# Keys and values of the context made beside the first scans instead of in the tail of a Mamba, MLP, attention and LoRA kernel

## The chip, the cores and the metric

The kernel runs on one core of a Trainium2 chip. The core has five engines with queues of their own: TensorE (PE, with weight loads shown as PEld), VectorE (DVE), ScalarE (ACT), GpSimd (POOL) and SyncE (SP), which here only issues transfers. The metric is the device time of one execution in microseconds (us). The profile is of one execution; L311 in it is the line of a helper through which most instructions go, so that groups are told apart by the names of their tiles.

## The reference

The input is x, 4 sequences of 1024 tokens and 512 channels (4096 tokens in all), and a context of 64 tokens for each sequence. One decoder layer with three parts is computed in float32, with a residual and a layer norm behind each part. Cut to what matters:

```python
h   = x + mamba(rmsnorm(x))                  # in_proj, conv, dt, B, C; the scan below; out_proj
mlp = silu(xn @ w1.T) * (xn @ w2.T) @ w3.T   # xn = rmsnorm(h)
x   = layernorm(x + h + mlp)
# scan of mamba, for 1024 inner channels d and 16 states n:
#   h[t] = exp(dt[t,d] * A[d,n]) * h[t-1] + dt[t,d] * B[t,n] * u[t,d];   y[t,d] = sum_n h[t] * C[t,n]
K = ctx @ Wk.T + bk;  V = ctx @ Wv.T + bv    # 16 heads of 32
Q = x @ Wq.T + bq;    qk = Q K^T
t = exp(clip(mlp3(mean qk, max qk, variance of softmax qk)))    # a temperature for each head
x = layernorm(x + (softmax(qk / (2 t)) V) @ Wo.T + bo)
x = layernorm(x + x @ W.T + b + top-2 mixture of 8 LoRA experts)
```

K and V hang on the context and on weights alone; nothing that the kernel computes of x goes into them.

## The kernel before

The 4096 tokens are 8 chunks of 512. Work on them comes in these stages:

1. `mamba_in`: for each chunk the rms norm, the input projections, the convolution, dt, B, C and the gate. Its outputs (dt, dt times u, u, the gate, B, C) go to device memory.
2. `scan_mlp`: the scans. A *group* is half a chunk's inner channels (4 tiles of 128), and a *step* k is one of the 16 states n of a group, so that there are 256 steps: group 0 is steps 0 to 15, group 1 steps 16 to 31. A step has four *quarters* (`quarter(k, q, other)`). In quarter q DVE runs the scan of tile q of step k, ACT the exponent for the scan two quarters later (`exp`), PE transposes 128 tokens of step k - 1 into a PSUM bank (`turn`), and the bank is multiplied by C (`times_c`): for some (n, t) DVE adds it to an accumulator `acc`; for the others ACT writes it to a tile of its own (`hc`, or `hz` in the first two groups), which POOL adds later, or PE adds when it transposes back (`join`). In quarters 0 and 1 POOL makes the products with B for step k + 1 (`times_b`, tile `hs`). SP loads the row b of step k + 2 at quarter 0. `exp` has two PSUM banks, `turn` three.
3. From step 40 on, an MLP stream for chunk 0 and the later chunks runs on PE in `other`'s place, at a fixed pace. The first four steps (EARLY_STEPS) have the end of `mamba_in` there; from step 4 to step 39 that place is empty (`lambda: None`).
4. After the last step comes the MLP of the last chunk (`last()`), advanced by `alone`, and woven with it, turn by turn, the generator `Attention.start`, which makes ready for attention: constants, keys, values, the query weights, and then the scores of the first blocks.
5. `Attention.run`: the attention and the LoRA part, 256 tokens at a time, in an order written out by hand (`CP`).

The order on PE, DVE, ACT and POOL is the order of the program wherever `pin` is used as `nc` (class `InOrder`), one such order for `mamba_in` and one for `scan_mlp`. What is issued through the plain `nc` (all of SP, and in `Attention.start` everything but the matmuls) is placed by the framework's scheduler. `at(d, phase, f)` lets f run d quarters later, at phase 0 (before the turn), 1 (after it), 2 (before the scan) or 3 (at the end).

The keys and values before: `Attention.start` loads the context twice side by side (ctx2), wk, wv and bv, 3.25 MB together. For each of four blocks of key channels PE makes four matmuls over 256 columns into `ps_k`, ACT adds the bias (`kf`), ACT rounds it to the high part and DVE subtracts for the low part (`split`, tile `ks`), SP stores both parts in device memory, and DVE sums it (`ksum`). For each of the four sequences PE makes four matmuls over 512 columns into `ps_v`, DVE adds the bias (`vf`), `split` makes the two parts (`vs`), and SP stores them. A float32 matmul shows as two records in the profile. The banks are those of the MLP (`mm`, three). In front of them in PE's order stands the output projection of the last chunk (`ps_o`), behind some of them the four `turn`s of its MLP (`ps_t`), which need the rms norm of that projection: `norm_h` on DVE, `norm_sq` on ACT, the reciprocal root on POOL (`norm_r`), and `norm_x` on ACT.

The tiles `hz` of the first two groups come from a pool `b_z` of 44 buffers. Group 0 takes 36 of them and group 1 takes 38, from its first state on.

Of the kernel before, what the change touches and what calls it, by code (L numbers as in the profile page):

```python
# [19 lines left out]
P = 128  # L20
B, L, D = 4, 1024, 512
N = B * L
KD = D // P
# [261 lines left out]
def open_pool(tc, name, bufs, **kw):  # L285
    return tc.tile_pool(name=name, bufs=bufs, reuse_waits="tile", **kw)
# [40 lines left out]
class Slots:  # L327
# [5 lines left out]
    def at(self, d, phase, f, *args):  # L333
        self.due.setdefault((self.now + d, phase), []).append(lambda: f(*args))
# [357 lines left out]
    return rest()  # L692


def scan_mlp(tc, cn, a, dr, before, bx, then):

# [7 lines left out]
    with ExitStack() as ctx, ExitStack() as sx:  # L704
# [8 lines left out]

        carry = cp.tile([P, KI, NS], F32, tag="carry", name="carry")
        pks, bs, cts, accs, hcs, uzs, firsts = {}, {}, {}, {}, {}, {}, {}
        zps = []

        class Step:

# [79 lines left out]
            def times_c(self, t):  # L799

                c = cts[self.c][:, t, self.n : self.n + 1]
                ps = self.ps.rearrange("p i d -> p (i d)")
                if self.n == 0:
                    acc = accs[self.g, t] = ap.tile([P, GJ * P], F32, tag="acc", name="acc")
                    nc.scalar.activation(acc, ps, AF.Copy, scale=c)
                elif (self.n, t) in self.by_add | self.by_turn:
                    acc = accs[self.g, t]
                    if self.g < 2 and (self.n, t) in self.by_turn:
                        hc = zps[0].tile([P, GJ * P], F32, tag="hz", name="hz")
                    else:  # L810
# [351 lines left out]
        assert next(before, 0) == 0  # L1162
        bx.close()
        with ExitStack() as zx:
            zps.append(zx.enter_context(open_pool(tc, "b_z", bufs=44, side="right")))
            zps.append(
                zx.enter_context(open_pool(tc, "b_zp", bufs=2, space=PSUM, side="right"))
            )
            for k in range(EARLY_STEPS, 2 * NS + 8):
                for q in range(GJ):  # L1170
                    quarter(k, q, lambda: None)
            turned[0] = 0
# [71 lines left out]
class Attention:  # L1244
# [11 lines left out]
    def constants(self, cp):  # L1256
# [31 lines left out]
            )  # L1288
        nc.gpsimd.memset(f32(self.kbd), 0.0)

    def start(self, ctx, pin, mm):

        self.pin, self.mm = pin, mm
        nc, a, dr, pvec = self.nc, self.a, self.dr, self.cn["pvec"]
# [6 lines left out]
        self.ksum = cp.tile([P, 4, B], F32, tag="ksum", name="ksum")  # L1301
        for _ in range(7):
            yield
        with ExitStack() as kx:
            kv = self.pool(kx, "c_kv", 1)
            ctx2 = kv.tile([P, KD, B, 2, SK], F32, tag="ctx2", name="ctx2")
            wk = kv.tile([P, KD, D], F32, tag="wk", name="wk")
            wv = kv.tile([P, KD, D], F32, tag="wv", name="wv")
            bv = kv.tile([P, D], F32, tag="bv", name="bv")
            for i in range(2):  # L1310
                nc.sync.dma_start(
                    ctx2[:, :, :, i], a["ctxT"].rearrange("p k (b s) -> p k b s", b=B)
                )
            nc.sync.dma_start(wk, a["wk"])
            nc.sync.dma_start(wv, a["wv"])
            nc.sync.dma_start(bv, a["bv"].partition_broadcast(P))
            nc.sync.dma_start(self.tw1, a["tw1"])
            nc.sync.dma_start(self.tw2, a["tw2"])
            nc.sync.dma_start(self.tb3, a["tb3"].partition_broadcast(P))
            self.constants(cp)  # L1320
            nc.vector.tensor_copy(self.tw3, self.tw2[:, 66:67].to_broadcast([64, P]))
            yield
            for hb in range(4):
                ps = mm.tile([P, T], F32, tag="mm", name="ps_k")[:, 0 : B * SK]
                ps = ps.rearrange("p (b s) -> p b s", s=SK)
                for k in range(KD):
                    pin.tensor.matmul(
                        ps, wk[:, k, hb * P : (hb + 1) * P], ctx2[:, k, :, 0],
                        start=k == 0, stop=k == KD - 1,
                    )  # L1330
                kf = kv.tile([P, B, SK], F32, tag="kf", name="kf", bufs=2)
                nc.scalar.activation(kf, ps, AF.Identity, bias=pvec[:, V_BK + hb : V_BK + hb + 1])
                ks = kv.tile([P, 2, B, SK], F32R, tag="ks", name="ks", bufs=2)
                split(nc, ks[:, 0], ks[:, 1], kf)
                for i in range(2):
                    nc.sync.dma_start(dr["k"][:, :, i, hb], f32(ks[:, i]))
                nc.vector.tensor_reduce(self.ksum[:, hb], kf, AX.X, ALU.add)
                if hb % 2:
                    yield
            for b in range(B):  # L1340
                ps = mm.tile([P, T], F32, tag="mm", name="ps_v")
                for k in range(KD):
                    pin.tensor.matmul(
                        ps, ctx2[:, k, b].rearrange("p i s -> p (i s)"), wv[:, k],
                        start=k == 0, stop=k == KD - 1,
                    )
                vf = kv.tile([P, D], F32, tag="vf", name="vf", bufs=2)
                nc.vector.tensor_tensor(vf, ps, bv, ALU.add)
                vs = kv.tile([P, 2, D], F32R, tag="vs", name="vs", bufs=2)
                split(nc, vs[:, 0], vs[:, 1], vf)  # L1350
                nc.sync.dma_start(dr["v"][b], f32(vs))
# [604 lines left out]
def build(tc, a, out):  # L1956
    nc = tc.nc
    with ExitStack() as ctx:
# [41 lines left out]
        scan_mlp(tc, cn, a, dr, before, bx, lambda pin, mm: att.start(ctx, pin, mm))  # L2000
        att.rest(ctx)
        att.run()

# [70 lines left out]
```

## Time and profile before

| | us |
|---|---|
| median of three runs | 3323.96 (3316.99 to 3324.38) |
| the profiled execution | 3321.16 |
| its span, first to last instruction | 3319.4 |
| PE busy | 2993.0 (90%) |
| DVE busy | 2867.0 (86%) |
| POOL busy | 2454.5 (74%) |
| ACT busy | 2043.6 (62%) |
| mean granted TensorE clock | 0.955 |

The page cuts the span into 40 slices of 83 us each and gives each engine's busy share of a slice in tenths. `mamba_in` fills about the first six slices, group 0 and 1 of the scans lie around slices 7 to 10, the scans with MLPs go to about slice 30, and then come the last MLP and attention. PEclk is the clock that TensorE was granted, in tenths of full speed. The page's chain, followed back from the last instruction, is 38% PE, 26% DVE and 10% POOL. An instruction in an answer of the trace is given with its start, its duration, engine, line, what it writes and reads, its shape, how many were merged, and in brackets the idle time of the engine in front of it and what ended that.

### The profile page before, as it was taken

What the parts mean: (1) busy time and instruction counts of PE and PEld (TensorE: products, weight loads), DVE (VectorE), ACT (ScalarE), POOL (GpSimd) and SP (SyncE); (2) the same over time, 40 slices, a digit from 0 to 9 for tenths busy, and PEclk for the clock granted to TensorE, in tenths of its full rate; (3) what the DMA queues carried; (4) which work ended last, traced back from release to release, by engine and by line L of the source; (5) the groups of instructions that cost most, each with busy time, mean ns of one, the idle gap of its engine ahead of it and who ended that gap; (6) DMA issues with size and microseconds to landing.
All of it is one profiled execution on the core that took longest, in us unless ns stands there. A gap on an engine that the chain in (4) does not pass through costs nothing.

```text
span 3319.4 us, 47302 instructions
## 1 busy us (share of the span) xinstructions
PE 2993.0 (90%) x15768; PEld 2366.4 (71%) x15768; DVE 2867.0 (86%) x4063; ACT 2043.6 (62%) x4000; POOL 2454.5 (74%) x2153
## 2 busy tenths in 40 slices
PE   7999894677899999999999998999999998999986
PEld 5767672565686786786786786786786887998875
DVE  6888887998999999999999999999983346889887
ACT  3778788775665566665566665566652336666642
POOL 1456547898999999999999999999972215667643
PEclk9999995678999999999999999999999999999998
DMA  4677745334666666666766765765757532112010
GB/s 161 221 260 241 256 175 173 99 111 166 210 207 193 216 203 191 222 203 188 230 196 184 238 190 183 241 191 179 234 171 231 161 108 93 52 39 65 30 39 32
DMA packets 478474, 562.79 MB, mean 170 GB/s; under 512 B 46006, under 2 KB 309814, under 8 KB 477974
## 3 DMA queue, kind: packets, MB, share of 16 engines
q1 hardware_dynamic: 464406, 526.21, 49.6%
q10 hardware_dynamic: 13824, 33.56, 2.9%
q8 instruction: 125, 2.05, 0.2%
q14 instruction: 119, 0.97, 0.1%
HBM read 430.18 MB, written 129.50 MB: 169 GB/s over the span
## 4 chain that ended last, share of the span: by engine, by line
PE 38%; DVE 26%; POOL 10%; issue 6%; ACT 5%; DMA 3%; SPq 0%; ACTq 0%; POOLq 0%; DVEq 0%
DVE hs L311 11%; PE ps_ab L311 10%; PE ps_h L311 5%; PE ps_o L311 5%; POOL hs L311 5%; PE ps_m L311 5%; DVE acc L311 5%; PE ps_s L311 3%; PE ps_b L311 2%; POOL acc L311 2%; DVE g L311 1%; ACT da L311 1%; PE ps_in L311 1%; PE ps_y L311 1%; PE ps_num L311 1%
## 5 line engine op out<-in xcount | busy, mean ns | idle before, releaser
L311 DVE TENSOR_TENSOR_SCAN hs<-da,hs 128x512 f32<-128x512 f32 x1024 | 1225.3, 1217 | 19.8 <-ACT da L311 19.4
L311 POOL TENSOR_TENSOR hs<-pk,b 128x1024 f32<-128x1024 f32 x512 | 1214.1, 2387 | 23.3 <-PE ps_h L311 14.9
L311 ACT ACTIVATE da<-pk,aneg 128x512 f32<-128x512 f32 x1024 | 706.2, 690 | 632.1 <-DVE hs L311 622.0
L311 PE MATMUL ps_ab<-xn,w 128*128 128x512 f32 x3072 | 832.6, 407 | 3.4 <-DVE xs L311 3.4
L311 PE MATMUL ps_h<-ident,hs 128*128 128x128 f32 x4096 | 693.0, 291 | 129.1 <-DVE hs L311 66.1
L311 PEld LDWEIGHTS ps_h<-ident,hs 128*128 128x128 f32 x4096 | 533.4, 148 | 371.0 <-DVE hs L311 112.2
L311 PEld LDWEIGHTS ps_ab<-xn,w 128*128 128x128 f32 x3072 | 547.8, 191 | 98.9 <-DVE xs L311 4.1
L311 DVE SCALAR_TENSOR_TENSOR acc<-ps_h,c,acc 128x512 f32<-128x512 f32 x598 | 439.8, 735 | 26.1 <-PE ps_h L311 20.7
L311 PE MATMUL ps_m<-w,gs 128*128 128x512 f32 x1536 | 418.4, 409 | 6.0 <-POOL gs L311 3.5
L311 POOL TENSOR_TENSOR acc<-acc,hc 128x512 f32<-128x512 f32 x232 | 298.9, 1288 | 68.3 <-ACT hc L311 67.1
L311 PEld LDWEIGHTS ps_m<-w,gs 128*128 128x128 f32 x1536 | 275.6, 192 | 55.4 <-POOL gs L311 5.5
L311 PE MATMUL ps_o<-wo,wy 128*128 128x512 f32 x512 | 247.1, 601 | 10.0 <-DMA wy<-y 8.8
L311 POOL TENSOR_TENSOR gs<-g,gs 128x512 fp32r<-128x512 f32 x128 | 164.9, 1288 | 79.8 <-ACT gs L311 79.5
L311 PE MATMUL ps_in<-xn,wu 128*128 128x512 f32 x768 | 217.5, 433 | 0.3 <-DVE xn L475 0.2
L311 PE MATMUL ps_in<-xn,wz 128*128 128x512 f32 x768 | 193.2, 400 | 8.2 <-DVE cv L311 4.1
L311 ACT ACTIVATE hc<-ps_h,c 128x512 f32<-128x512 f32 x288 | 193.1, 671 | 3.8 <-PE ps_h L311 3.8
L311 PEld LDWEIGHTS ps_in<-xn,wu 128*128 128x128 f32 x768 | 147.4, 193 | 58.8 <-issue 23.8
L311 POOL TENSOR_TENSOR pt<-pw,pt 128x512 fp32r<-128x512 f32 x48 | 67.3, 1402 | 161.8 <-ACT pt L311 133.8
L311 PEld LDWEIGHTS ps_in<-xn,wz 128*128 128x128 f32 x768 | 143.2, 189 | 43.4 <-ACT q L311 4.6
L311 DVE SCALAR_TENSOR_TENSOR g<-g,ps_ab 128x512 f32<-128x512 f32 x128 | 87.4, 683 | 85.3 <-ACT g L311 84.7
L311 DVE SCALAR_TENSOR_TENSOR cv<-ps_in,pvec,cv 128x509 f32<-128x509 f32 (+2 forms) x192 | 143.3, 746 | 4.8
L311 POOL TENSOR_TENSOR q<-qf,q 128x256 fp32r<-128x256 f32 x64 | 47.6, 744 | 127.4 <-ACT q L311 127.3
(251 smaller groups left out, 4982.6 us busy)
## 6 DMA issues: line engine op xcount, KB each, us to landing
w<-w SPq DMA_DIRECT2D x384, 512.0 KB, 5.3
b<-b SPq DMA_DIRECT2D x256, 256.0 KB, 4.3
pk<-pk SPq DMA_DIRECT2D x64, 512.0 KB, 5.8
w<-pt SPq DMA_DIRECT2D x48, 512.0 KB, 3.1
pk<-z SPq DMA_DIRECT2D x64, 256.0 KB, 2.3
pk<-u SPq DMA_DIRECT2D x32, 512.0 KB, 3.7
pk<-r SPq DMA_DIRECT2D x32, 512.0 KB, 4.6
pk<-q SPq DMA_DIRECT2D x32, 512.0 KB, 5.3
```

Of the source, the lines that this page charges most:

```text
L311: ins = f(*args, **kw)
```

## The change

The generator `keys_values` is new. It does the work described above for keys and values, with its transfers, in `scan_mlp` in the place of `other`, one call in each quarter of steps 4 to 14. It issues through `pin`, so that its instructions stand in the scans' order. It has a PSUM bank (`b_kq`, one buffer) and a pool (`b_kv`) of its own, which are closed before step 15; `b_z` gets 36 buffers in place of 44, and a pool `b_z2` of 8, opened at step 15, serves the first 8 `hz` tiles of group 1.

The calls, counted from 0 at step 4, quarter 0: loads of the context in calls 0 and 1, of the four parts of wk in 2 to 5, bv in 6; a block of keys in calls 8, 11, 14 and 17; the four parts of wv, in the space of wk, in 20 to 23; and a sequence's values in calls 24, 28, 32 and 36, two of its four matmuls in that call and two in the next. The low parts are subtracted on POOL, where DVE did it before. Transfers: two of the context, eight of weights (two before), bv, eight stores of keys and four of values. `Attention.start` keeps as many turns as before, six of them now empty, and the rest of its work.

```diff
-        zps = []
+        zps, joined = [], [0, 0]
@@ times_c
                     if self.g < 2 and (self.n, t) in self.by_turn:
-                        hc = zps[0].tile([P, GJ * P], F32, tag="hz", name="hz")
+                        joined[self.g] += 1
+                        hz = zps[2 if self.g and joined[1] <= 8 else 0]
+                        hc = hz.tile([P, GJ * P], F32, tag="hz", name="hz")
@@ scan_mlp
-            zps.append(zx.enter_context(open_pool(tc, "b_z", bufs=44, side="right")))
+            zps.append(zx.enter_context(open_pool(tc, "b_z", bufs=36, side="right")))
...
-            for k in range(EARLY_STEPS, 2 * NS + 8):
+            with ExitStack() as kx:
+                kv = kx.enter_context(open_pool(tc, "b_kv", bufs=1, side="right"))
+                kq = kx.enter_context(open_pool(tc, "b_kq", bufs=1, space=PSUM, side="right"))
+                extra = beside(kv, kq, pin, at)
+                for k in range(EARLY_STEPS, NS - 1):
+                    for q in range(GJ):
+                        quarter(k, q, lambda: next(extra, None))
+                assert next(extra, 0) == 0
+            zps.append(zx.enter_context(open_pool(tc, "b_z2", bufs=8, side="right")))
+            for k in range(NS - 1, 2 * NS + 8):
                 for q in range(GJ):
                     quarter(k, q, lambda: None)
@@ class Attention
+    def keys_values(self, kp, kv, mm, pin, at):
+        nc, a, dr, pvec = pin, self.a, self.dr, self.cn["pvec"]
...
+        def key_bias(hb, ps, kf):
+            kf.append(kv.tile([P, B, SK], F32, tag="kf", name="kf"))
+            nc.scalar.activation(
+                kf[0], ps, AF.Identity, bias=pvec[:, V_BK + hb : V_BK + hb + 1]
+            )
+        def key_hi(kf):
+            kf.append(kv.tile([P, 2, B, SK], F32R, tag="ks", name="ks"))
+            nc.scalar.copy(kf[1][:, 0], kf[0])
+        def key_sum(hb, kf):
+            nc.vector.tensor_reduce(self.ksum[:, hb], kf[0], AX.X, ALU.add)
+        def key_lo(hb, kf):
+            f, s = kf
+            nc.gpsimd.tensor_tensor(s[:, 1], f, f32(s[:, 0]), ALU.subtract)
+            for i in range(2):
+                nc.sync.dma_start(dr["k"][:, :, i, hb], f32(s[:, i]))
+        def value_bias(ps, vf):
+            vf.append(kv.tile([P, D], F32, tag="vf", name="vf"))
+            nc.vector.tensor_tensor(vf[0], ps, bv, ALU.add)
+        def value_hi(vf):
+            vf.append(kv.tile([P, 2, D], F32R, tag="vs", name="vs"))
+            nc.scalar.copy(vf[1][:, 0], vf[0])
+        def value_lo(b, vf):
+            f, s = vf
+            nc.gpsimd.tensor_tensor(s[:, 1], f, f32(s[:, 0]), ALU.subtract)
+            nc.sync.dma_start(dr["v"][b], f32(s))
...
+        for hb in range(4):
+            ps = mm.tile([P, T], F32, tag="kv", name="ps_k")[:, 0 : B * SK]
...
+            kf = []
+            at(1, 1, key_bias, hb, ps, kf)
+            at(2, 1, key_hi, kf)
+            at(2, 2, key_sum, hb, kf)
+            at(2, 3, key_lo, hb, kf)
+            for _ in range(3):
+                yield
...
+        for b in range(B):
+            ps = mm.tile([P, T], F32, tag="kv", name="ps_v")
+            for k in range(KD):
+                nc.tensor.matmul(
+                    ps, ctx2[:, k, b].rearrange("p i s -> p (i s)"), w[k],
+                    start=k == 0, stop=k == KD - 1,
+                )
+                if k == 1:
+                    yield
+            vf = []
+            at(1, 2, value_bias, ps, vf)
+            at(2, 1, value_hi, vf)
+            at(2, 3, value_lo, b, vf)
+            for _ in range(3):
+                yield
@@ Attention.start
-            ctx2 = kv.tile([P, KD, B, 2, SK], F32, tag="ctx2", name="ctx2")
-            wk = kv.tile([P, KD, D], F32, tag="wk", name="wk")
-            wv = kv.tile([P, KD, D], F32, tag="wv", name="wv")
-            bv = kv.tile([P, D], F32, tag="bv", name="bv")
...
-            nc.sync.dma_start(wk, a["wk"])
-            nc.sync.dma_start(wv, a["wv"])
-            nc.sync.dma_start(bv, a["bv"].partition_broadcast(P))
...
             yield
-            for hb in range(4):
-                ps = mm.tile([P, T], F32, tag="mm", name="ps_k")[:, 0 : B * SK]
...
-            for b in range(B):
-                ps = mm.tile([P, T], F32, tag="mm", name="ps_v")
...
+            for _ in range(6):
                 yield
```

More of the change, by code (lines that the diff above doesn't have):

```diff
@@ L692, in mamba_in, with scan_mlp @@
     return rest()
-def scan_mlp(tc, cn, a, dr, before, bx, then):
+def scan_mlp(tc, cn, a, dr, before, bx, beside, then):
     pin = InOrder(tc, tc.nc)
@@ L1289, in constants, with load @@
         nc.gpsimd.memset(f32(self.kbd), 0.0)
+    def keys_values(self, kp, kv, mm, pin, at):
+        nc, a, dr, pvec = pin, self.a, self.dr, self.cn["pvec"]
+        ctx2 = kv.tile([P, KD, B, 2, SK], F32, tag="ctx2", name="ctx2")
+        self.ksum = kp.tile([P, 4, B], F32, tag="ksum", name="ksum")
+        bv = kv.tile([P, D], F32, tag="bv", name="bv")
+        def load(w, k):
+            t = kv.tile([P, D], F32, tag=f"w{k}", name=f"wkv{k}")
+            nc.sync.dma_start(t, a[w][:, k])
+            return t
+        def key_bias(hb, ps, kf):
[23 more added lines that the diff above has]
+            nc.sync.dma_start(dr["v"][b], f32(s))
+        for i in range(2):
+            nc.sync.dma_start(
+                ctx2[:, :, :, i], a["ctxT"].rearrange("p k (b s) -> p k b s", b=B)
+            )
+            yield
+        w = []
+        for k in range(KD):
+            w.append(load("wk", k))
+            yield
+        nc.sync.dma_start(bv, a["bv"].partition_broadcast(P))
+        for _ in range(2):
+            yield
+        for hb in range(4):
+            ps = mm.tile([P, T], F32, tag="kv", name="ps_k")[:, 0 : B * SK]
+            ps = ps.rearrange("p (b s) -> p b s", s=SK)
+            for k in range(KD):
+                nc.tensor.matmul(
+                    ps, w[k][:, hb * P : (hb + 1) * P], ctx2[:, k, :, 0],
+                    start=k == 0, stop=k == KD - 1,
+                )
+            kf = []
[4 more added lines that the diff above has]
+            for _ in range(3):
+                yield
+        for k in range(KD):
+            w[k] = load("wv", k)
+            yield
+        for b in range(B):
+            ps = mm.tile([P, T], F32, tag="kv", name="ps_v")
+            for k in range(KD):
+                nc.tensor.matmul(
+                    ps, ctx2[:, k, b].rearrange("p i s -> p (i s)"), w[k],
+                    start=k == 0, stop=k == KD - 1,
+                )
+                if k == 1:
+                    yield
+            vf = []
[3 more added lines that the diff above has]
+            for _ in range(3):
+                yield
@@ L1291, in start @@
     def start(self, ctx, pin, mm):
         self.pin, self.mm = pin, mm
-        nc, a, dr, pvec = self.nc, self.a, self.dr, self.cn["pvec"]
+        nc, a = self.nc, self.a
         cp = self.pool(ctx, "c_c", 1)
@@ L1300, in start @@
         self.tb3 = cp.tile([P, 1], F32, tag="tb3", name="tb3")
-        self.ksum = cp.tile([P, 4, B], F32, tag="ksum", name="ksum")
         for _ in range(7):
@@ L1305, in start @@
             kv = self.pool(kx, "c_kv", 1)
-            ctx2 = kv.tile([P, KD, B, 2, SK], F32, tag="ctx2", name="ctx2")
-            wk = kv.tile([P, KD, D], F32, tag="wk", name="wk")
-            wv = kv.tile([P, KD, D], F32, tag="wv", name="wv")
-            bv = kv.tile([P, D], F32, tag="bv", name="bv")
[L1310 to L1313, printed above, removed]
-            nc.sync.dma_start(wk, a["wk"])
-            nc.sync.dma_start(wv, a["wv"])
-            nc.sync.dma_start(bv, a["bv"].partition_broadcast(P))
             nc.sync.dma_start(self.tw1, a["tw1"])
@@ L1322, in start @@
             yield
-            for hb in range(4):
-                ps = mm.tile([P, T], F32, tag="mm", name="ps_k")[:, 0 : B * SK]
[L1325 to L1339, printed above, removed]
-            for b in range(B):
-                ps = mm.tile([P, T], F32, tag="mm", name="ps_v")
[L1342 to L1351, printed above, removed]
+            for _ in range(6):
                 yield
@@ L1999, in build @@
         att = Attention(tc, cn, a, dr, out)
-        scan_mlp(tc, cn, a, dr, before, bx, lambda pin, mm: att.start(ctx, pin, mm))
+        scan_mlp(
+            tc, cn, a, dr, before, bx, lambda *args: att.keys_values(cp, *args),
+            lambda pin, mm: att.start(ctx, pin, mm),
+        )
         att.rest(ctx)
```

## The prediction

> **What bounds the kernel now.** I read the busy table and the forty slices first, then 20 us windows of the two stretches that the change touches, then their timelines, and last the tiles of the moved work. In the page, slices 7 to 10 are the first scans: DVE and POOL are near full and the granted TensorE clock is low. From slice 31 on PE is full while DVE and POOL have room: the tail.
>
> ```profile
> PE   7999894677899999999999998999999998999986
> DVE  6888887998999999999999999999983346889887
> PEclk9999995678999999999999999999999999999998
> ```
>
> The windows (start:end, length, then busy time and count of PE, PEld, DVE, ACT, POOL, the granted clock, DMA share, GB/s) show the place the work goes to, and the place it leaves.
>
> ```profile
> 600.00:620.00 20.00, 14.37 (x63) 9.99 (x64) 19.97 (x21) 16.82 (x32) 19.11 (x10) 0.65 0.16 54
> 620.00:640.00 20.00, 15.29 (x63) 10.36 (x62) 19.97 (x20) 17.22 (x32) 18.58 (x8) 0.59 0.24 75
> 660.00:680.00 20.00, 16.43 (x140) 15.01 (x139) 18.72 (x21) 13.84 (x25) 18.63 (x11) 1.00 0.38 112
> ...
> 2540.00:2560.00 20.00, 18.85 (x72) 11.98 (x71) 8.51 (x17) 10.23 (x20) 4.28 (x15) 1.00 0.89 267
> 2560.00:2580.00 20.00, 18.61 (x72) 12.54 (x70) 6.29 (x11) 4.13 (x7) 3.04 (x2) 1.00 0.70 207
> ```
>
> In the scans DVE is busy 19.97 of 20 us: whatever is put into DVE's queue, as work or as a wait, lengthens the program by itself. In the tail PE has the least room. Counting scans from the first (536.7), step 4 starts at 572.9, step 6 at 595.1, and from step 7 (600.3) four steps take 20.6 us, 5.15 each: four scans at a pitch of 1.15 and one addition of 0.65. The timeline of two such steps:
>
> ```profile
> 622.56 8.05 DVE L311 TENSOR_TENSOR_SCAN hs<-da,hs 128x512 f32<-128x512 f32 x7
> 625.25 3.40 PE L311 MATMUL ps_h<-ident,hs 128*128 128x128 f32 x12 [0.58 <-ACT hz L311]
> 630.52 0.73 DVE L311 SCALAR_TENSOR_TENSOR acc<-ps_h,c,acc 128x512 f32<-128x512 f32 x1
> 633.77 0.66 PE L311 MATMUL ps_h<-ident,hs 128*128 128x128 f32 x4 [0.49 <-ACT hz L311]
> ```
>
> A turn (four transposes) costs PE 1.13 us at half clock (3.40/3) and about 0.52 at full clock (eight in 1.04 in the tail, below). The timeline of the tail:
>
> ```profile
> 2518.05 24.30 PE L311 MATMUL ps_o<-wo,wy 128*128 128x512 f32 x56 [1.22 <-DMA wo<-in_w_out_dram]
> 2542.19 7.07 PE L311 MATMUL ps_k<-ctx,wk 128*128 128x256 f32 x32
> 2549.09 7.03 PE L311 MATMUL ps_v<-wv,ctx 128*128 128x512 f32 x16
> 2555.96 1.04 PE L311 MATMUL ps_t<-ident,hn 128*128 128x128 f32 x8
> 2559.46 3.70 PE L311 MATMUL ps_v<-wv,ctx 128*128 128x512 f32 x8 [0.68 <-DVE xn L311]
> 2562.59 3.33 PE L311 MATMUL ps_ab<-xn,w 128*128 128x512 f32 x12
> 2565.76 3.60 PE L311 MATMUL ps_v<-wv,ctx 128*128 128x512 f32 x8
> ```
>
> All keys and half the values lie between the output projection and the turns of the last MLP, where PE would otherwise wait for the norm; the other half stands in front of products.
>
> **What leaves the tail.** PE loses 7.1 + 14.3 = 21.4 us of ps_k and ps_v, ACT, DVE 4.4 and 5.0 us that had room anyway, SP 17 transfers. The 21.4 us is not the gain, because the norm does not get faster. The timeline has the last ps_o ending at 2542.35, POOL's reciprocal root ready at 2548.11 and hn scaled on ACT by four instructions from 2548.14:
>
> ```profile
> 2547.91 0.20 POOL L311 TENSOR_TENSOR nr<-rs_r,rs_w 128x4 f32<-128x4 f32 x1
> 2548.14 1.95 ACT L311 ACTIVATE hn<-hn,nr 128x512 f32<-128x512 f32 x3 [1.39 <-POOL nr L311]
> ```
>
> Without the kf in between, the fourth ends at 2550.8 and the turns start there rather than at 2555.96. PE then stood idle for 8.5 us. After an idle stretch of 5.6 us before 2802.96 the windows show a clock of 0.50 and full clock again at about 2807, 4.3 us later. So the turns run at half clock: four of 1.1 us, the fourth also waiting for the first bank (ACT 0.69, DVE 0.75), 4.5 us in all, and products start at about 2555.35 instead of 2562.59: 7.2 us. The second pair of values goes whole: 3.0 us (2565.76 to 2568.79). The wait of 1.22 us for wo lies in a stretch where DMA is 0.96 busy with, among others, the 3.25 MB of context and weights; I take 0.8 of it. Tail: 7.2 + 3.0 + 0.8 = 11.0 us gained; 8 if the clock comes back later, 13.2 if the turns run at full clock (4.5 becomes 2.7, and all of the 1.22 goes). After this PE is full to 2740, so the gain is kept. tw loads, constants and wq stay, with as many empty turns in between as before.
>
> The Trainium skill ("TensorE: Matmul & The Clock Gate", section "Why this matters for your kernels") advises against PE-idle gaps over about 3 us between bursts, which is what the change makes here; its window of about 3.4 us in place of the 4.3 us seen would leave the tail's gain some 0.5 us larger.
>
> **What comes into the scans.** Keys begin at step 6, quarter 0 (three quarters each), values at steps 10 to 13, each from quarter 0, in the scans' own fixed order on each engine.
>
> ```profile
> L1337 DVE TENSOR_REDUCE ksum<-kf x4: 419/420/420, 2544.6 to 2551.4; 128x4 f32<-128x256 f32 x4
> L1348 DVE TENSOR_TENSOR vf<-ps_v,bv x4: 682/688/692, 2554.7 to 2569.4; 128x512 f32<-128x512 f32 x4
> ```
>
> 1. DVE's own work: 4 x 0.42 + 4 x 0.69 = 4.4 us, all on the path.
> 2. Waits for values. A value is 8 PE records, 3.5 us at full clock (16 in 7.03), half in quarter 0 behind turn 0, half in quarter 1 behind turn 1; DVE's vf stands ahead of scan 2. The last transpose of turn 0 needs the last scan of the step before. From the step's start: turn 0 ends at 0.3, half a value at 2.05, turn 1 at 2.6, the other half at 4.35. DVE is there after two scans, 2.30, or 2.95 where its addition is in the first two quarters (steps 10 and 11; not 12 and 13). Waits: 1.4 + 1.4 + 2.05 + 2.05 = 6.9 us. Behind the waiting vf stand two scans, and behind them ACT's exponents and POOL's next step.
> 3. The clock. The rows at 0.65 and 0.59 say the first value meets half clock: half a value 3.5, so 3.9, turn 1 at 5.0, and, the clock rising on the way, the end near 7.2 rather than 4.35: +2.9. The other three find PE busy three quarters of the step; the row at 660, with 16.43 of 20, holds 1.00. Bounds: 0, and all four wholly at half clock, 4 x 4.15 = 16.6.
> 4. Waits for keys. The first key (1.75 us, 3.5 at half clock) is behind turn 0 of step 6, where PE is late already; ACT's bias waits for it in front of the exponent for scan 3, and turn 1, for which DVE's addition waits, is behind it. PE gets through it at about 600.0 and turn 1 at 600.6; DVE, at 597.3, waits 3.3. The other three fall where PE is ahead: 0.3 each from ACT, which has 16.82 to 17.22 of 20 already. 4.2; bounds 1 and 8.
> 5. ACT's cast of each value, 0.62, is in front of an exponent with some 0.4 to spare: 4 x 0.25 = 1.0 (0 to 2.5).
> 6. POOL: 4 x 0.74 + 4 x 1.29 = 8.1 us. It has 0.5 us a step free over 11 steps and the steps grow by more than the rest: nothing, or 2.7 if they don't.
> 7. SP: 2 ctx, 4 wk, 4 wv, bv, 8 k and 4 v, 23 transfers, pass loads of b and pk. SP is held at 588.27 and 593.40 by stores of r; ctx took 2.5 us each to issue and 9.6 to land, wk 8.3. Loads put behind the first store land at about 601, for a key wanted at 598: I take 2 (0 to 6). b is loaded two steps, 10.3 us, ahead and lands in 3.3.
>
> The bank and the 8 buffers of hz in a pool of their own take no instruction; as many as before serve, and b_z2, which takes over the space of the keys and values, is first wanted in step 18, four steps after the last value: nothing; were that store late, one wait of its landing, 3.1. Sum: 4.4 + 6.9 + 2.9 + 4.2 + 1.0 + 2.0 = 21.4 us lost, 14 to 30; the scans have no later slack that I see. Net 21.4 - 11.0 = 10.4 us slower. Against the profiled execution (3321.16, span 3319.4) that is 3331.6; the median of the runs, 3323.96, lies 2.8 above it: **3334**.
>
> The Trainium skill (same page, "PE-mode transpose") says that transposes don't engage the full clock. The window at 660 shows transposes alone at 1.00, so the row decides. By the rule turn 1 would keep 1.1 us beside warm matmuls and each value would end some 0.7 us later, 2.8 in all.
>
> **Rivals.** *Half clock throughout, or late loads:* items 3 and 7 at their upper parts, 10 and 5 more: net +25, 3349. For it speaks the fall of the clock within 4 us whenever PE is half idle (0.59 on average); against it the row at 660. Chance 0.22.
> *Waits hidden:* the scans' delay is taken back where all engines stand idle for 8.76 us on the load of wy near 800. Net +1.6, 3325.6. Against it: that load follows a store of the second group, which is late by as much. Chance 0.12.
> *Faster:* DVE is not what limits the scans; POOL, at 18.6 to 19.1 of 20 with 4.66 us of products in each 5.15, does, and DVE's records only look closed. Then DVE and PE take the new work for nothing and the tail's 11 us stays: 3313. It decides if the scans lose less than 1 us. Against it: DVE's pitch is that of its own instructions back to back. Chance 0.12.
> *Forecast* 0.54, own range +2 to +20 (3326 to 3344), three fifths of it above +10.
>
> **How the numbers follow.** About 0.3%, 10 us, is what a measurement can tell from no change. Slower: 0.22 + 0.6 x 0.54 = 0.54. Same: 0.4 x 0.54 + 0.12 = 0.34. Faster 0.12. The range goes from 3315, which leaves out most of the faster case (0.08), to 3352, which leaves out about 0.1.
>
> **What would show it.** Steps 10 to 13 some 7.5 to 9 us long, DVE idle in front of vf with ps_v as releaser; a gap in front of the first key's sum; the last scan of step 15 some 21 us later; clock at 1.00 in steps 11 to 13. In the tail a PE gap of about 8.5 us in front of the first turn, half clock in the turns, and the first product some 7 to 8 us sooner after the last ps_o. Wrong if steps 10 to 13 stay under 6.5 us, if the first key waits for a load, or if the norm is followed by PE sooner than 8 us.

## The result

The changed kernel takes 3343.18 us (median of 6 runs, 3337.38 to 3345.22) against 3320.35 us of the kernel before in the same session (6 runs, 3316.99 to 3324.38). The ratio is 1.0059, with a 95% interval of 1.0049 to 1.0069: slower by 19.6 us by the ratio, 22.8 by the medians. The two measures can differ by some us, as here. The forecast was 3334 us, 10.4 us slower, in a range of 3315 to 3352. The direction is right and the time lies inside the range, but the loss is about twice the forecast's.

The profiled execution of the changed kernel is 3345.22 us long, with a span of 3343.4 us: 24.0 us over the span of before. The forty slices of its page:

```profile
PE   6999994687899999999999999999899998999986
DVE  6888987698899999999999999999992345888887
PEclk9999995777899999999999999999999998999998
```

Slice 8 (585 to 669 us) is the new thing: DVE falls there from 9 to 6. Most of the loss lies in it.

**Where the time went.** Every scan, norm and product of the two traces can be matched by its number, and the start in the changed kernel less the start in the kernel before gives its delay. The sums in the table are DVE's additions of the last MLP's output (tile `h`), the write is DVE's of tile `x` from `ps_lo`:

| point | time before | delay | gained or lost on the way |
|---|---|---|---|
| step 6, first scan | 595.1 | -1.6 | |
| step 9, first scan | 610.6 | 16.1 | 17.7 lost: keys |
| step 10, first scan | 615.7 | 17.0 | 0.9 lost: last key |
| step 14, first scan | 636.3 | 29.8 | 12.7 lost: values |
| step 32, first scan | 735.4 | 30.0 | 0.3 lost |
| last norm of the MLP (hn) | 2542.4 | 32.3 | 2.2 lost, in small parts |
| first sum of the last MLP (h) | 2605.2 | 18.6 | 13.6 gained: tail |
| last sum of the last MLP (h) | 2749.5 | 18.6 | 0 |
| third write of the last stage (x) | 2867.9 | 23.0 | 4.4 lost |
| end | 3319.4 | 24.0 | 1.0 lost |

**The keys.** The timeline of the changed kernel around the first key (start, length, engine, work; in brackets how long the engine had stood idle, and for what):

```profile
593.03 1.73 SPq L354 DMA_DIRECT2D pk<-q  x2
594.81 4.30 SPq L1349 DMA_DIRECT2D ctx<-in_ctxT_dram  x2
599.16 4.16 SPq L1313 DMA_DIRECT2D wkv<-in_wk_dram  x4
603.37 0.43 SPq L1357 DMA_DIRECT2D bv<-in_bv_dram  x1
...
605.10 3.87 PE L311 MATMUL ps_k<-ctx,wkv 128*128 128x256 f32 x8 [10.62 <-DMA wkv<-in_wk_dram]
609.00 0.47 ACT L311 ACTIVATE kf<-ps_k,pvec 128x256 f32<-128x256 f32 x1 [12.81 <-PE ps_k L311]
609.68 0.75 DVE L311 SCALAR_TENSOR_TENSOR acc<-ps_h,c,acc 128x512 f32<-128x512 f32 x1 [13.88 <-PE ps_h L311]
```

SP gets to the context only at 594.81, behind stores of r and q. The first of the four parts of wk lands at 605.0, 5.8 us behind its issue, and TensorE starts at 605.10; the other parts land up to 607.3, and the key has to wait for each of them too. TensorE stands 10.62 us in front of the key, with the next turn of the scan's output behind it in its order; ScalarE stands 12.81 us for the bias; DVE, which needs that turn for its addition, 13.88 us. Windows of the same stretch (the columns are those of the prediction: length, then busy time and count of PE, PEld, DVE, ACT, POOL, the clock, DMA share, GB/s):

```profile
595.00:605.00 10.00, 0.00 (x0) 0.00 (x0) 0.80 (x1) 1.19 (x2) 3.95 (x2) 0.50 1.10 273
605.00:615.00 10.00, 8.54 (x38) 6.60 (x39) 5.17 (x7) 4.45 (x10) 4.54 (x3) 0.78 0.43 135
615.00:625.00 10.00, 7.47 (x43) 5.65 (x42) 8.06 (x10) 8.57 (x18) 6.95 (x5) 1.00 0.60 133
625.00:635.00 10.00, 6.11 (x20) 3.91 (x21) 9.17 (x9) 7.03 (x15) 6.83 (x4) 0.57 0.40 112
635.00:645.00 10.00, 8.39 (x33) 4.45 (x32) 6.58 (x8) 4.86 (x10) 5.46 (x4) 0.92 0.15 53
645.00:655.00 10.00, 8.29 (x28) 4.36 (x27) 5.28 (x5) 6.66 (x12) 8.59 (x5) 0.83 0.35 125
655.00:665.00 10.00, 7.11 (x36) 4.30 (x34) 8.29 (x10) 5.61 (x10) 6.78 (x4) 1.00 0.25 79
```

From 595 to 605 TensorE does nothing, DVE 0.80, ACT 1.19 and POOL 3.95 us of 10, and DMA is full (share 1.10, 273 GB/s). The waits of DVE between 590 and 692 us (total, times, longest):

```profile
DVE acc L311 <- PE ps_h L311: 16.1, 2, 13.9
DVE vf L311 <- PE ps_v L311: 7.4, 4, 3.5
DVE ksum L311 <- ACT kf L311: 1.6, 2, 0.9
DVE hs L311 <- ACT da L311: 1.5, 3, 0.8
```

These are 26.6 us, and with the 4.4 us of DVE's own four sums and four biases 31.0: nearly the whole of the 31.4 us that the scans lose (DVE's waits in the kernel before are 1.3 us in the same stretch). Each value has its wait (0.97, 1.48, 3.48 and 1.48 us), and the 2.2 us of the first line beside the 13.9 belong to the first value, behind whose first half a turn came late at half clock.

**The tail.** The timeline of the changed kernel behind the output projection:

```profile
2571.44 3.17 PE L311 MATMUL ps_o<-wo,wy 128*128 128x512 f32 x7
...
2579.89 0.20 POOL L311 TENSOR_TENSOR nr<-rs_r,rs_w 128x4 f32<-128x4 f32 x1
2580.12 2.56 ACT L311 ACTIVATE hn<-hn,nr 128x512 f32<-128x512 f32 x4 [3.96 <-POOL nr L311]
2580.89 4.94 PE L311 MATMUL ps_t<-ident,hn 128*128 128x128 f32 x16 [6.28 <-ACT hn L311]
2585.62 2.57 PE L311 MATMUL ps_ab<-xn,w 128*128 128x512 f32 x10
```

TensorE has nothing between the last ps_o and the first turn: 6.28 us idle. From the first of the sixteen transposes to the first product it is 4.7 us, and products start 11.0 us behind the last ps_o instead of 20.2.

### The profile page after: what moved, and what is told of

Read it like the earlier page. It is cut to its first block, busy times and chain, and to the rows that moved or that the text cites. A ratio compares the mean times of both kernels' runs of the same rounds, so it can differ in the third digit from the quotient of the medians.

```text
span 3343.4 us, 47306 instructions
## 1 busy us (share of the span) xinstructions
PE 3005.1 (90%) x15768; PEld 2376.5 (71%) x15768; DVE 2862.9 (86%) x4055; ACT 2044.4 (61%) x4000; POOL 2465.3 (74%) x2161
## 3 DMA queue, kind: packets, MB, share of 16 engines
q8 instruction: 125, 2.05, 0.3%
## 4 chain that ended last, share of the span: by engine, by line
PE 42%; DVE 29%; POOL 10%; ACT 7%; issue 7%; DMA 4%; SPq 1%; ACTq 0%; DVEq 0%; POOLq 0%
DVE hs L311 11%; PE ps_ab L311 9%; PE ps_h L311 6%; PE ps_o L311 5%; PE ps_in L311 5%; DVE acc L311 5%; PE ps_m L311 4%; POOL hs L311 4%; PE ps_s L311 3%; PE ps_b L311 2%; DVE g L311 2%; POOL acc L311 2%; PE ps_y L311 1%; DVE cv L311 1%; ACT da L311 1%
## 5 line engine op out<-in xcount | busy, mean ns | idle before, releaser
L311 DVE TENSOR_TENSOR_SCAN hs<-da,hs 128x512 f32<-128x512 f32 x1024 | 1220.2, 1210 | 19.6 <-ACT da L311 19.5
```

The lines of the kernel that those rows point to most:

```text
L311: ins = f(*args, **kw)
```

## The experiments

The theory after the result: the parts add up. Late loads cost about 11 us of the 31, waits behind the bursts of keys and values some 16, DVE's own work 4.4, and the tail gives 13.6 back. Each run below takes one or more of these away. The delays quoted come from matching each trace with that of before, as in the table; "the scans lose" is the delay at the first scan of step 20 less that of step 6, and the last column counts from the very first scan instead. The kernel before ran beside the changed kernel at 3320.35 us, beside the first four kernels (loads early, tail alone, scans alone and values later, with 8, 11, 4 and 5 runs) at 3320.08 (18 runs) and beside the last four, which have 11 runs each, at 3321.41 (33 runs, 3317.03 to 3327.89).

| run | median us | ratio to before | 95% interval | scans lose us | from the first scan |
|---|---|---|---|---|---|
| changed kernel | 3343.18 | 1.0059 | 1.0049 to 1.0069 | 31.4 | 31.5 |
| loads early | 3326.63 | 1.0023 | 1.0013 to 1.0033 | 20.3 | 15.3 |
| tail alone | 3323.75 | 1.0012 | 1.0003 to 1.0021 | 0.6 | 0.7 |
| scans alone | 3351.95 | 1.0098 | 1.0084 to 1.0112 | 30.5 | 30.5 |
| values later | 3338.62 | 1.0058 | 1.0044 to 1.0071 | 31.2 | 31.2 |
| loads early, values later | 3327.26 | 1.0018 | 1.0009 to 1.0027 | 17.9 | 15.3 |
| loads early, two buffers | 3327.98 | 1.0020 | 1.0011 to 1.0029 | 18.3 | 17.7 |
| tail alone, copies moved | 3324.26 | 1.0005 | 0.9996 to 1.0013 | 0.0 | 0.0 |
| loads early, spread | 3314.76 | 0.9977 | 0.9968 to 0.9986 | 5.5 | 0.8 |

The two columns part only in the runs with early loads, because there the steps ahead of step 6 run otherwise too. Steps 4 and 5 together take 19.0 to 21.5 us there and 22.2 before, and one product of DVE in them (`r<-r,q`) takes 2.2 to 5.7 us where it took 5.8. The first four steps take 34.4 us in three of these runs and 38.5 with two buffers, against 36.2. Why is not known; so a distance of 2 us between two of these runs is not safe unless the waits show it too.

### Loads early

The context, wk and bv are loaded ahead of step 0 into a pool of their own; the rest is as in the changed kernel, with empty turns where the loads were.

```diff
+        kl = lx.enter_context(open_pool(tc, "b_kl", bufs=1))
+        early = beside(None, None, pin, at, kl)
+        next(early)                      # ctx2, wk, bv: loaded here
         for k in range(EARLY_STEPS):
...
-        for i in range(2):
-            nc.sync.dma_start(ctx2[:, :, :, i], ...)
-            yield
-        for k in range(KD):
-            w.append(load("wk", k))
-            yield
+        for _ in range(8):
+            yield
```

> The changed kernel, but the context rows, wk and bv are loaded ahead of step 5 into a space of their own; the rest is as in the changed kernel. Theory L (the first key waits for its loads, which were issued at 595 to 605 us behind other work of SP): the gap of about 10 us in which DVE, TensorE and POOL stand still near 600 us goes, the scans lose about 20 us to the kernel before instead of 31, and the time ends 9 to 13 us under the changed kernel's, some 11 us above the kernel before. Rival K (the gap is the price of the key's matmuls at half clock in TensorE's order, and the loads only run beside it): the gap moves but stays, the scans lose 28 to 31 us, and the time is within 4 us of the changed kernel's.

The scans lose 20.3 us and the ratio falls to 1.0023, some 12 us under the changed kernel's: theory L. It stays 7.6 us above the kernel before by the ratio, where 11 were expected; the shorter steps 4 and 5, which the count from step 6 leaves out, are 3.2 us here. The timeline around the loads and the first key:

```profile
518.15 1.87 SPq L1322 DMA_DIRECT2D ctx<-in_ctxT_dram  x2
520.07 3.76 SPq L1311 DMA_DIRECT2D wkv<-in_wk_dram  x4
...
592.67 3.62 PE L311 MATMUL ps_k<-ctx,wkv 128*128 128x256 f32 x8
596.09 1.70 PE L311 MATMUL ps_h<-ident,hs 128*128 128x128 f32 x12
596.33 0.47 ACT L311 ACTIVATE kf<-ps_k,pvec 128x256 f32<-128x256 f32 x1 [1.73 <-PE ps_k L311]
...
596.95 0.75 DVE L311 SCALAR_TENSOR_TENSOR acc<-ps_h,c,acc 128x512 f32<-128x512 f32 x1 [2.74 <-PE ps_h L311]
```

The key takes 3.62 us (3.87 in the changed kernel, where it also waited for parts of wk), but it starts when TensorE reaches it, and DVE waits 2.74 us behind it in place of 13.88. The delay from step 6 to step 10 falls from 18.6 to 7.8 us: the late loads cost 10.8, and DVE's first wait alone falls by 11.1. What is left of the keys, 7.8 us, holds 1.7 of DVE's own sums. The values cost what they did (four waits of 7.4 us in both).

### The two halves alone

Tail alone: no key or value is made, and the two arrays that the tail reads are filled by copies. Scans alone: keys and values in the scans, and the tail's function of the kernel before, which makes them again.

```diff
 # tail alone: in keys_values
+        nc.gpsimd.memset(self.ksum, 0.0)
+        return
 # and ahead of the first stage
+        nc.sync.dma_start(dr["k"]..., a["wk"]...)
+        for b in range(B):
+            nc.sync.dma_start(dr["v"][b], a["wv"][:, 0:2])

 # scans alone: Attention.start as in the kernel before
```

> The changed kernel without the making of keys and values: none of their loads, matmuls, biases, casts, sums and stores is done anywhere; the two arrays in DRAM that the tail reads are filled by copies at the start, and the key sums are zero (so the output is not the reference's, and this part of the computation is left out). It holds what the tail gains, and what the new spaces alone cost the scans. Theory: the scans run as in the kernel before (their starts within 2 us), the tail gains 13.6 us as in the changed kernel, and the time is 10 to 14 us under the kernel before. Rival (the scans lose time by the divided space of the joined tiles, 36 and 8 in place of 44): the scans lose over 3 us and the gain is under 10. Rival (the tail's gain is eaten by the later gap in which the clock falls): 8 to 10 us under.

> The scans as in the changed kernel, with keys and values made in them; and the tail of the kernel before, which makes them a second time. Theory (the parts add): the scans lose 31 us, the tail gains nothing, the time is 30 to 33 us above the kernel before, some 10 us above the changed kernel. Rival (part of the loss at the scans is given back in the MLP stretch or the tail): under 25 us above the kernel before.

Scans alone came out as the theory had it: 0.98% slower, 32.5 us, with the scans at 30.5 and a tail that gives nothing. Against the changed kernel's 0.59% this leaves 12.9 us (0.39%) for the tail in timed runs, beside the 13.6 of the traces. So the parts add, and the gain of the tail does reach the end. (In the other profiles of the changed tail the same stretch gives 12.3 to 13.7.)

The tail alone missed its expectation, by its own fault. The scans do keep their pace (0.6 us lost), so the divided space of the joined tiles, 36 and 8, costs nothing, and the tail's step gives 13.5 us; but everything starts 14.0 us late. The copies stand in SP's order ahead of the first weights. I moved them to where the tail's preparation begins:

```diff
     def start(self, ctx, pin, mm):
+        nc.sync.dma_start(dr["k"]..., a["wk"]...)
+        for b in range(B):
+            nc.sync.dma_start(dr["v"][b], a["wv"][:, 0:2])
```

> As the run that holds the tail's part alone (no key or value made, key sums zero, output not the reference's), but the copies that fill the two arrays stand behind the scans, where the tail's preparation begins, and not at the start, where they held back the first loads by 14 us. Theory: the scans keep the pace of the kernel before within 1 us, the tail gains 13.5 to 14.5 us, and the time is 8 to 14 us under the kernel before. Rival (the tail's gain is given back later, by the clock's fall in the next gap of TensorE): 4 to 8 us under.

They were issued at the start again, as SP's timeline of that run shows:

```profile
7.42 0.61 SPq L1355 DMA_DIRECT2D k<-in_wk_dram  x1
8.12 2.55 SPq L1359 DMA_DIRECT2D v<-in_wv_dram  x3
10.79 0.51 SPq L293 DMA_DIRECT2D pw<-in_w_in_dram  x1
11.35 0.49 SPq L1359 DMA_DIRECT2D v<-in_wv_dram  x1
```

Lines 1355 and 1359 are in the tail's function; these copies, which depend on no earlier work of the program, did not stay where they are written. The first scan is 14.9 us late, so as a total this run says nothing clean either. Counted from the first scan on, its profiled execution is 12.9 us better than before (delay 14.9, at the end 2.0), and that of the first version 8.1 (14.0 and 5.9). I leave the tail's worth at the 12.9 us between the two timed kernels above.

### Values later

Each value's bias and halves come two quarters later behind its matmuls, and a value has six quarters in place of four, so that the stretch runs on to step 15.

```diff
-            at(1, 2, value_bias, ps, vf)
-            at(2, 1, value_hi, vf)
-            at(2, 3, value_lo, b, vf)
-            for _ in range(3):
+            at(3, 2, value_bias, ps, vf)
+            at(4, 1, value_hi, vf)
+            at(4, 3, value_lo, b, vf)
+            for _ in range(5):
                 yield
```

> The changed kernel with the bias, the first half and the second half of each value put two quarters (one half step) later behind its matmuls, and six quarters in place of four for each value; the loads and keys are as in the changed kernel. Theory V (DVE arrives at the value's bias before TensorE has finished the value): the four waits of DVE for a value, 7.4 us in all, and the 2.2 us behind them go; the scans lose 21 to 24 us in place of 31, and the time ends 7 to 10 us under the changed kernel's. Rival W (another wait takes the place: TensorE's order is what is late, and DVE then waits for the sums of the scan's own output): the scans lose 28 us or more and the time is within 4 us of the changed kernel's.

The waits for values are gone, and the time is not: 1.0058, and the scans lose 31.2 us. DVE's waits of this run in the same stretch, ScalarE's for a store, and the two lines of the timeline where that one ends:

```profile
DVE acc L311 <- PE ps_h L311: 20.6, 4, 14.3
DVE hs L311 <- ACT da L311: 3.7, 2, 2.9
DVE ksum L311 <- ACT kf L311: 1.5, 2, 0.9
...
ACT vs L311 <- DMA v<-vs: 2.6, 1, 2.6
```

```profile
676.50 0.62 ACT L311 CAST vs<-vf 128x512 fp32r<-128x512 f32 x1 [2.56 <-DMA v<-vs]
...
677.74 2.58 DVE L311 TENSOR_TENSOR_SCAN hs<-da,hs 128x512 f32<-128x512 f32 x2 [2.90 <-ACT da L311]
```

Rival W is right (by the ratio the time is within 0.4 us of the changed kernel's). 14.3 of the 20.6 us are the first key's (13.9 before). The other waits for ps_h rise from 2.2 to 6.3 us and those for da from 1.5 to 3.7: of the 7.4 us of waits for vf 6.3 came back under other names. The half value of two k (four records, 1.9 us at full clock) still stands in TensorE's order in front of the turn that DVE's addition needs. And with one buffer the fourth value's halves wait for the store of the third, 2.6 us on ScalarE and 2.9 on DVE.

> The early loads and the later value steps together (each alone: 20.3 and 30.6 us lost at the scans, against 31.4 to 29.8 in the changed kernel). Theory W2 (the wait for a value only changes its name: the value's matmuls go two at a time into TensorE's order and the scan's own turned outputs stand behind them, and the one buffer of the halves waits for its store): the scans lose 17 to 21 us to the kernel before, and the time is within 3 us of the one with early loads alone, 5 to 9 us above the kernel before. Rival V2 (the return of the waits came from the late start only): the scans lose 10 to 13 us and the time is 0 to 3 us above the kernel before.

With early loads as well (a run of both edits), the scans lose 17.9 us and the ratio is 1.0018, beside 20.3 and 1.0023 for early loads alone, and 15.3 in both when counted from the first scan: theory W2. It is not the late start that made the waits come back.

### Two buffers

Early loads, and two buffers for ks and vs.

```diff
-            kf.append(kv.tile([P, 2, B, SK], F32R, tag="ks", name="ks"))
+            kf.append(kv.tile([P, 2, B, SK], F32R, tag="ks", name="ks", bufs=2))
-            vf.append(kv.tile([P, 2, D], F32R, tag="vs", name="vs"))
+            vf.append(kv.tile([P, 2, D], F32R, tag="vs", name="vs", bufs=2))
```

> Early loads as before, and two buffers in place of one for the halves of keys and values. With one buffer ScalarE waited 0.7, 1.6 and 1.4 us for the store of the last key's halves, and the scan behind it 1.3 us for its decay. Theory D: those three waits go, and the scans lose 1 to 3 us less than with early loads alone (17 to 19 us). Rival (ScalarE has the slack and the waits cost nothing): the same 20 us within 0.5.

The scans lose 18.3 us, 2.0 less than with early loads alone: theory D by the trace. In the time (1.0020 against 1.0023) two microseconds can't be seen, and counted from the first scan this run loses 2.4 us more and not less. What stands on firm ground is the waits: DVE's for the decay and ScalarE's for a store with early loads alone, and then DVE's with two buffers:

```profile
DVE hs L311 <- ACT da L311: 2.3, 4, 1.3
...
ACT ks L311 <- DMA k<-ks: 3.7, 3, 1.6
```

```profile
DVE vf L311 <- PE ps_v L311: 7.4, 4, 3.2
DVE acc L311 <- PE ps_h L311: 4.6, 3, 2.5
DVE ksum L311 <- ACT kf L311: 1.4, 2, 0.7
DVE hs L311 <- ACT da L311: 0.7, 2, 0.5
```

The wait for ScalarE's decay falls from 2.3 to 0.7, and ScalarE's waits for k's stores, 3.7 us in three before, are gone. The waits behind the bursts stay: 7.4 and 4.6, beside 7.4 and 4.7.

### Spread

Early loads and two buffers; a key has two of its matmuls in each of two quarters, a value one in each of four; a value's bias comes two quarters behind its last matmul, a key's sum one quarter later. The keys begin five quarters sooner, in step 4.

```diff
-        for _ in range(8):                            # ahead of the keys
+        for _ in range(3):
             yield
...
             for k in range(KD):                       # key
                 nc.tensor.matmul(ps, w[k]..., ctx2[:, k, :, 0], ...)
+                if k == 1:
+                    yield
...
-            at(2, 2, key_sum, hb, kf)
+            at(3, 2, key_sum, hb, kf)
...
             for k in range(KD):                       # value
                 nc.tensor.matmul(ps, ctx2[:, k, b]..., w[k], ...)
-                if k == 1:
+                if k < KD - 1:
                     yield
-            at(1, 2, value_bias, ps, vf)
-            at(2, 1, value_hi, vf)
-            at(2, 3, value_lo, b, vf)
-            for _ in range(3):
+            at(2, 2, value_bias, ps, vf)
+            at(3, 1, value_hi, vf)
+            at(3, 3, value_lo, b, vf)
+            for _ in range(3 + b // (B - 1)):
```

> Early loads, two buffers for the halves, keys with two matmuls in a quarter and values with one (six quarters a value), the value's bias two quarters behind its last matmul, a key's sum one half step later. Theory T (of the 20 us that the scans still lose with early loads, 4.4 are DVE's own work, and 5.7, 7.4, 1.6 and some 1 are waits behind matmuls that come in bursts): the waits go, the scans lose 5 to 9 us, the tail keeps its 13.7, and the time is 3 to 8 us under the kernel before, the first version that is faster than it. Rival W3 (the matmuls of keys and values cost TensorE's order the same however they are spread): the scans lose 15 to 20 us and the time is 4 to 8 us above the kernel before.

The scans lose 5.5 us, and the ratio is 0.9977 (0.9968 to 0.9986): 6.7 us under the kernel before by the medians, the only version that beats it. That is as theory T had it; the tail gives 12.4 us in this profile, not 13.7. All of DVE's waits from 590 to 692, and two windows while values are made:

```profile
DVE hs L311 <- ACT da L311: 1.8, 3, 0.8
DVE acc L311 <- PE ps_h L311: 1.3, 1, 1.3
```

```profile
612.00:622.00 10.00, 8.80 (x41) 4.91 (x41) 10.00 (x12) 7.98 (x15) 10.00 (x6) 1.00 0.25 70
622.00:632.00 10.00, 8.05 (x39) 4.51 (x38) 10.00 (x11) 9.06 (x18) 8.88 (x6) 1.00 0.32 104
```

The matmuls are the same in number and form, and DVE is full again; TensorE, with one piece of 1.0 us between two turns, holds 1.00 through both windows. So the waits were not the price of the matmuls as such, and rival W3 falls. Of the 5.5 us that remain some 3.3 are DVE's own (three sums and four biases, from each start to the next; the first key's sum lies ahead of the count), and 2.3 are waits, 1.34 of them behind the first key.

Several things were moved in this run: the matmuls are in smaller pieces, the biases come later behind them, and the keys start sooner. Its 12.8 us against the run with two buffers are not divided among them. Later biases without smaller pieces took only 2.4 us off (20.3 to 17.9 with early loads), but that run had one buffer, and ScalarE waited 4.0 us in it for a store of v; later biases with two buffers were not run. The 12.8 come from both halves of the stretch: 6.3 us between steps 6 and 11 (9.3 against 3.0), 6.6 between steps 11 and 20 (9.0 against 2.4). The keys begin before step 6 in this version; there the distance of the two traces stays at 3.4 to 3.7 us, so nothing is lost ahead of the count.

## Why the prediction was right, and where it was wrong

**What bounds the scans** was right: whatever goes into DVE's queue lengthens the program by itself. Its waits and work account for 31.0 of 31.4 us. One of the prediction's own signs against it came all the same: the first key waited for a load. The rival that POOL was the limit, and the one that the delay is taken back near 800, fall: the delay is 29.8 at step 14 and 32.3 at the end of the MLP.

**Term by term** (predicted, then measured):

| term | predicted | measured | by |
|---|---|---|---|
| 1. DVE's own work | 4.4 | 4.4 | its durations |
| 2 and 3. waits for values, clock | 6.9 + 2.9 | 7.4 + 2.2 | DVE's waits |
| 4. waits for keys | 4.2 | 6.1 | 7.8 with early loads, less four sums |
| 5. ScalarE's cast of a value | 1.0 | 0.4 | the rest of 12.7 at the values |
| 6. POOL | 0 | 0 | the rest |
| 7. late loads | 2.0 (0 to 6) | 10.8 | 18.6 less 7.8 with early loads |
| scans | 21.4 | 31.4 | |

Four of the five rows at the scans that were not zero came within 2 us. Item 7 is the step that failed. It said: "Loads put behind the first store land at about 601, for a key wanted at 598: I take 2 (0 to 6)." TensorE wanted the key at 594.5, at a pace 1.6 us ahead of before, so the wish was set 2 us too late and, at that pace, the landing 6 us too soon. What was wrong is the place of the loads in SP's order. The first store of r was issued at 586.67 and over at 587.2; the loads came not behind it but behind the second store of r (591.81), a row b and two stores of q, at 594.81. From there the parts of wk landed 10.2 to 12.5 us later, which is what the prediction allowed from the first store (588.3 in the kernel before) to 601. The bound of 6 had the same fault. With 10.8 in its place the sum is 21.4 + 8.8 = 30.2 at the scans, against 31.4.

The sum of items 2 and 3 (9.8 forecast, 9.6 measured) is partly luck. Item 3 charged 2.9 us of half clock to the first value and let the other three run at full clock. In the trace the first value costs 3.2 us (2.2 and 0.97) where 4.3 were forecast, and the third 3.48 where it was 2.05: TensorE's clock was down again in the window from 645 (0.83). The sign that was named, a clock of 1.00 in steps 11 to 13, did not hold. One row at 16.43 busy us of 20 and 1.00 did not carry so far: the kernel before has 17.49 of 20 at a clock of 0.74 in the window from 640 to 660.

Item 4's first wait was well placed: 3.3 forecast, 2.74 with early loads. What was missed there is the one buffer of the halves: k's stores queue among the loads of wv on SP, ScalarE waits for them, and a scan waits for ScalarE (with two buffers DVE's waits for the decay fall by 1.6 us).

**The tail** gave 13.6 us where 11.0 were forecast (8 to 13.2). The mechanism was as described; the size of the gap was off. The prediction let the turns start when the fourth hn was scaled; the trace starts them 0.8 us after the first scaling began. So TensorE was idle for 6.28 us and not 8.5 (under 8 was named as a sign against it), and the products came 9.2 us sooner and not 7.2. With the 3.0 us of the second pair of values this is 12.2 of the 13.6; 0.44 more is a wait for xq that is gone, and the rest is not assigned. (The wait for wo is gone too, but lies ahead of the point from which the 13.6 are counted.) The turns did run at half clock, 4.7 us for four (clock 0.50 from 2580 to 2584, 0.59 in the next 2 us), where 4.5 was forecast. The clock came back 4.7 us after TensorE started again; the 4.3 us that the prediction read from the row at 2806 of the kernel before come out as 4.7 there too, by the row's 0.58.

The Trainium skill ("TensorE: Matmul & The Clock Gate", section "Why this matters for your kernels") warns of gaps of TensorE longer than some 3 us. This gap of 6.28 us did bring the clock down, as the page has it; by the prediction's figures (2.7 us for the turns at full clock) that cost some 2 us of what the tail could have gained. At the scans the rows show a fall without such a gap: from 620 to 655 TensorE was never idle for more than 1.93 us at a stretch, and the clock was 0.57 to 0.92 in the three windows from 625 to 655. With the matmuls in single pieces it was 0.95 to 1.00 in the windows from 592 to 642.

**"After this PE is full to 2740, so the gain is kept"** held as far as it goes: nothing is lost between the first and the last sum of the MLP. Behind that it does not. Between the last sum and the third write of the last stage the profiled execution lost 4.4 us more. TensorE has a gap there in both kernels, for POOL's et; the timelines, before and after:

```profile
2768.23 0.51 PE L311 MATMUL ps_num<-et,vp 128*128 128x256 f32 x2 [3.19 <-POOL et L311]
```

```profile
2786.86 0.66 PE L311 MATMUL ps_num<-et,vp 128*128 128x256 f32 x2 [3.21 <-POOL et L311]
```

The windows behind it, before and after:

```profile
2770.00:2774.00 4.00, 2.12 (x19) 1.85 (x17) 2.58 (x3) 1.59 (x5) 1.87 (x3) 1.00 0.63 208
...
2782.00:2786.00 4.00, 3.17 (x17) 2.75 (x18) 0.95 (x2) 3.75 (x11) 4.00 (x5) 1.00 0.33 95
```

```profile
2788.00:2792.00 4.00, 4.00 (x26) 3.97 (x26) 1.46 (x3) 1.18 (x3) 0.88 (x2) 0.69 0.72 241
...
2800.00:2804.00 4.00, 4.00 (x20) 4.00 (x20) 0.72 (x2) 1.34 (x5) 1.42 (x3) 0.50 0.13 33
```

The same gap let the clock fall in one and not in the other, and in the changed kernel it fell a second time some 10 us later. The loss goes with the clock over all ten profiles. In the 30 us behind the gap the granted clock averages 1.00 before; 0.94 in three others (early loads, scans alone, tail alone with the copies moved), which lose 0.3 to 1.4 us in this stretch; 0.89 in three (both edits, tail alone, two buffers), which lose 0.2 to 2.6; and 0.83 in three (changed kernel, values later, spread), which lose 3.5 to 5.5. This is not shown to be a consequence of the change: the run with the scans alone, whose tail is that of before, has the fall too. What makes the clock fall or hold at this gap stays open. The few microseconds are of the size of the scatter of the kernel before between runs (3317.03 to 3327.89).

From the forecast's 10.4 us to the profile's 24.0 it is +10.0 at the scans, -2.6 in the tail, +2.5 in small parts of the stretch with MLPs, +5.4 behind the last MLP and -1.6 from a first scan that came sooner. The range held the result although one term was off by 8.8 us and one stretch behind the tail was not in the sum at all.

Of the rivals, "half clock throughout, or late loads" was half right: its late loads came, with 8.8 us more where it had 5, and its half clock came only in parts. The two together made its 25 us look near the profile's 24.0 for a reason that is partly wrong.

## What to carry to other kernels

A transfer that is moved into a full stretch is priced from the time when its queue really reaches it, behind everything that stands in the queue's order, and by the landing of the whole set that the first use needs; the cure that worked here is to issue it a stage earlier. Work that was put into the order of a half-idle engine cost by what had to wait behind it, not by its own length alone: keys and values in pieces of one microsecond between turns, with later biases, cost the scans 5.5 us, and in bursts 18.3. When one wait is taken away, look for what stands behind it in the same queue before counting the gain.

## What the runs showed of the hardware

- A gap of TensorE of 3.2 us (3.16 to 3.21 in the rows read) was followed within 2 us by a clock of 0.50 in eight of ten profiled kernels here; in the other two (the kernel before, and early loads alone) it stayed at 1.00 there. At this length the outcome isn't given by the program's text.
- TensorE's clock fell to 0.57 over 10 us (625 to 635 in the changed kernel) though it was never idle for more than 1.93 us at a stretch.
- Six loads (two of 512 KB and four of 256 KB), issued from 594.81 us behind stores of q, had landed only at 605.0 to 607.3, as far as wk goes; DMA moved 273 GB/s from 595 to 605, and TensorE and DVE stood. Issued at 518 us, ahead of the scans, the same loads made no matmul wait.
- Four copies of 0.5 MB and one of 1 MB issued between 7.4 and 11.8 us, among the first weights, went with a first scan of the program 14 to 15 us later (two profiles; it moves by 2 us at most in the others).
